# An earlier place in the queue for three transposing steps and one copy of a selective scan

## The chip, the cores and the metric

The kernel runs on one core of a Trainium2 chip. The metric is the time of one execution on the device in microseconds; the kernel before is given as the median of three runs.

## The reference

Two layers act on an input x of shape (2, 48, 48, 768) in float32, so on two images of 2304 tokens. Layer 1 adds neighbourhood attention (12 heads of 64, windows of 7 by 7) to x. Layer 2 adds a selective scan that is run over the tokens forwards and backwards:

```python
# layer 2, one direction; u, delta: (batch, 1536, 2304); A: (1536, 16); Bm, Cm: (batch, 16, 2304)
def step(h, inp):
    d_t, B_t, C_t, u_t = inp
    dA = jnp.exp(d_t[..., None] * A)
    h = dA * h + (d_t * u_t)[..., None] * B_t[:, None, :]
    y = jnp.einsum('bdn,bn->bd', h, C_t)
    return (h, y)
...
y = _selective_scan(x, delta, A, Bm, Cm) + x * Dp[None, :, None]
return y * jax.nn.silu(z)
...
out = jnp.einsum('bdl,cd->blc', out_f + out_b, out_proj_w)
```

Around it stand group norms, an input projection to x and z, a convolution of four taps, small projections that give delta, B and C, and the output projection.

## The kernel before

**Units.** The scan is cut into 288 units, numbered x = 0 to 287 in the order of execution: for each image, the forward direction and then the backward one; in each, 6 chunks of 384 tokens; in each chunk, 12 tiles of 128 channels (the change's title calls such units tiles). Units 0 to 71 are image 0 forwards, 72 to 143 image 0 backwards, 144 to 215 and 216 to 287 the same of image 1. `scan` writes the steps of one unit, and its inner `group` those of each of the 4 groups of 4 states:

1. *fill* (L1224): hb = u times B, 4 states side by side in one buffer `hb`, on VectorE or on GpSimd, whichever is free first for groups 1 to 3 (group 0 has no choice);
2. *exponentials* (L1246, ScalarE) into one of two PSUM buffers `da`;
3. *scans* (L1257, VectorE), two instructions a group, in place in `hb`;
4. *product* (L1272, GpSimd): hb times C, in place;
5. *add_up* (L1289, TensorE): 12 transposes that add the 4 states into one PSUM bank `py`. Only when they have run is `hb` free for another fill. There are seven `hb` buffers.

Each unit begins in `py` with *direct* (L1305, three transposes of x times D) and ends with a copy to `yt` (L1315, ScalarE). There is one `py`, so the next unit's *direct* waits for that copy. In the backward direction *sums* (L1342) transposes the forward result `yl` and `yt` back into one PSUM bank `yb` of the kind `mm`, of which there are two; VectorE multiplies it by the gate (L1352).

**Jobs.** All other work (attention, projections, norms, x_proj) is cut into jobs that are placed beside the scan. The attention of image 0 alone runs ahead of it. A projection is issued in parts of three products (L382), into the same two `mm` banks.

**The planner.** Nothing is ordered by hand. Every step is given to `Order.add` with an engine, an estimated duration and a *key*, its due place counted in units: a step of unit x has a key between about x - 1.4 and x + 1.4, and a job has a key that says beside which unit it should run. `Order.run` then plays the program through on its own clocks and, for each engine, takes the next step from those that are ready and whose buffers are free:

```python
                    rank = (max(t + over, free[e] + 150.0), x.first)
                    if pick is None or rank < pick[0]:
                        pick = rank, t, x
```

Here `t` is when the step could start, `free[e]` when the engine is free. All that could start within 150 ns of the engine's being free tie, and the lowest `x.first` goes ahead. It is set in `Order.add`:

```python
        x.then, x.ready, x.tail, x.first = [], 0.0, self.TAIL[eng], key - early
```

With `early` at 0 a job that is late (its key is lower than that of the unit now being scanned) goes ahead of a step of the scan. `EARLY = 20` is already given to the steps that make delta. The order that comes out is the order of issue on each engine, fixed when the program is built. A step with `alt` (the fill) may go to either engine, so a different order elsewhere can change the split. Where TensorE would stand idle for over 800 ns within a unit, transposes of a constant (L1489) are put in.

Keys that matter below, for image 0: the input projection of chunk i has keys from 9(i-1)-4 to 9(i-1)+8, its gate part for chunk 0 (`mm_z`) from 41 to 47, and the backward x_proj (`mm_xd`) from 44 to 55. For image 1: the attention has keys 50 to 118, the input projection of its first chunk 118 to 128, and its scan begins at unit 144. The output projection of image 0 has keys 188 to 212.

Of the kernel before, what the change touches and what calls it, by code (L numbers as in the profile page):

```python
# [43 lines left out]
SG = 4  # L44
# [49 lines left out]
class Order:  # L94
# [15 lines left out]
    @staticmethod  # L110
    def cells(uses):
        for x in uses:
            buf, parts = x if isinstance(x, tuple) else (x, range(x.parts))
            for p in (parts,) if isinstance(parts, int) else parts:
                yield buf, p
# [130 lines left out]
def tile_kernel(  # L246
# [3 lines left out]
    nc = tc.nc  # L250
# [57 lines left out]
    def cols(l0, cl, k0=0, nk=1):  # L308

        c0, c1 = l0 // CW, (l0 + cl) // CW  # L310
        return [k * NCW + c for k in range(k0, k0 + nk) for c in range(c0, c1)]
# [7 lines left out]
    def sb(tag, shape, n, parts=1):  # L319
        return Buf(f"{tag}_{n}", wk, shape, tag, BUFS.get(tag, 1), parts)  # L320

    def ps(tag, n):
        return Buf(f"{tag}_{n}", psum, [P, 512], tag, BUFS.get(tag, 1))
# [5 lines left out]
    def add(eng, ns, fn, key, r=(), w=(), job=False, size=0, after=None, early=0, alt=None, due=False, opens=None):  # L329

        news = [x[0] if isinstance(x, tuple) else x for x in w]

        def issue():
            for v in news:
                if v.ap is None:
                    v.ap = v.pool.tile(v.shape, F32, tag=v.tag, name=v.name, bufs=v.bufs)
            fn()

        if eng == "PE":

            ns *= 1.04 if key < 0 else 1.05
        return order.add(eng, ns, issue, key, r, w, job, size, after, early, alt, due, opens)
# [4 lines left out]
    def act(n, pointers=0):  # L347
        return 60 + 90 * pointers + n * 0.833

    def dve(n):  # L350
        return 55 + n * 1.042
# [695 lines left out]
    def x_proj(b, back, l0, cl, key):  # L1047

        n = f"{b}_{back}_{l0}"
        w = sb("xpw", [P, ND, XD], n)  # L1050
        u = staged(us[back][b], l0, cl, f"u{n}", key, w, par[back]["xpT"])
        acc = ps("mm", f"xd_{n}")
        product(acc, cl, [(w, k, 0) for k in range(ND)], [(u, k, 0) for k in range(ND)], key, XD)
        xd_out(b, back, l0, cl, n, acc, key)
# [124 lines left out]
    def scan(ch, k, x, dlj, duj, vt):  # L1179

        q, b, back, l0, cl, bc = (ch[v] for v in ("q", "b", "back", "l0", "cl", "bc"))
        at = x
# [8 lines left out]
        if k == 0 and ch["first"]:  # L1191
# [10 lines left out]
            early=EARLY,  # L1202
        )

        nt = -(-cl // P)
        tb = [slice(t * cl // nt, (t + 1) * cl // nt) for t in range(nt)]
        tp = cl // nt
        py = ps("py", n)

        def group(g):  # L1210
            m = f"{n}_{g}"
            now = at + 0.25 * g
            hb = sb("hb", [P, SG * W], m, SG + 1)
            body = (hb, range(SG))
            kept = lambda o: state[:, k, 2 * SG * g + o : 2 * SG * (g + 1) + o].rearrange(
                "p (j e) -> p j e", e=2
            )
            was = zero if ch["first"] else kept(0) if back else kept(1)

            def first():
                by, on = (dus[:, ju, :], nc.gpsimd) if filled.eng == "POOL" else (du[:, :W], nc.vector)
                on.tensor_mul(  # L1224
                    cells(hb, SG), by.unsqueeze(1).to_broadcast([P, SG, W]), bc[g].ap
                )

            if k == 0 or not ch["first"]:
                add(
                    "ACT", 98, lambda: nc.scalar.copy(bc[g][:, :, ends], was), now - 0.4,  # L1230
                    [(state, k * NSG + g)], [(bc[g], 1)], early=EARLY,
                )
            on = {"DVE": dve(SG * W), "POOL": SG * W * 2.2 + 20}
            main, other = ("DVE", "POOL") if g in (0, 1) else ("POOL", "DVE")
            filled = add(
                main, on[main], first, now - (0.35 if main == "POOL" else 0.1),
                [du, duj, bc[g]], [hb], after=marks.get(marks["n"] - 6),
                alt=(other, on[other]) if g in (1, 2, 3) else None,
            )

            def step(j):
                i = g * SG + j
                da = das[j // 2 % 2]
                add(
                    "ACT", act(cl, 1) + 45,
                    lambda: nc.scalar.activation(  # L1246
                        cells(da, 2)[:, j % 2, h], dl[:, jd, c], AF.Exp, scale=q["A"][:, k, i : i + 1]
                    ),
                    now + 0.06 * j - 0.06, [dlj], [(da, j % 2)], due=True,
                )  # L1250

            def two_steps(j):
                da = das[j // 2 % 2]
                at2 = (slice(None), slice(j * W, (j + 2) * W))
                mark = add(
                    "DVE", (4 * W + 42) / 0.96,
                    lambda: nc.vector.tensor_tensor_scan(  # L1257
                        flip(hb[at2]), flip(da[:, : 2 * W]), flip(hb[at2]), 0.0, ALU.mult, ALU.add
                    ),
                    now + 0.06 * j, [da], [(hb, (j, j + 1, SG))],  # L1260
                )
                marks[marks["n"]] = mark
                marks["n"] += 1

            for j in range(0, SG, 2):
                step(j)
                step(j + 1)
                two_steps(j)

            add(  # L1270
                "POOL", SG * cl * 2.03 + 10,
                lambda: nc.gpsimd.tensor_mul(  # L1272
                    cells(hb, SG)[:, :, h], cells(hb, SG)[:, :, h], bc[NSG + g][:, :, c]
                ),
                now + 0.25, [body, bc[NSG + g]], [body],
            )
            if not ch["final"]:
                add(
                    "ACT", 90,
                    lambda: nc.scalar.copy(  # L1280
                        kept(0)[:, :, 1:2], cells(hb, SG)[:, :, leaves : leaves + 1]
                    ),
                    now + 0.3, [body, (hb, SG)], [(state, k * NSG + g)],
                )

            def add_up():
                for j in range(SG):
                    for t in range(nt):
                        nc.tensor.matmul(  # L1289
                            py[:tp, t * P : (t + 1) * P], cells(hb, SG)[:, j, h][:, tb[t]], ident,  # L1290
                            start=False,
                            stop=g == NSG - 1 and j == SG - 1 and t == nt - 1,
                            is_transpose=True, skip_group_check=True,
                        )

            add(
                "PE", SG * nt * 109 + 60, add_up, now + 0.45, [body, py], [py],
                opens=False if g == NSG - 1 else None,
            )

# [6 lines left out]
                    is_transpose=True, skip_group_check=True,  # L1307
                )

        add("PE", nt * 109 + 60, direct, at + 0.3, [vt], [py], opens=True)  # L1310
        for g in range(NSG):
            group(g)
        yt = sb("yt", [P, CL], n)
        w, y0 = nt * P, l0
        add("ACT", act(w), lambda: nc.scalar.copy(yt[:tp, :w], py[:tp, :w]), at + 1.22, [py], [yt])  # L1315
        here = cols(l0, cl, k)
        if not back:
            add(
# [8 lines left out]
        yl, zs = (sb(v, [P, CL], n) for v in ("yl", "zs"))  # L1327
# [9 lines left out]
        yb = ps("mm", f"yb_{n}")  # L1337
# [7 lines left out]
                        skip_group_check=True,  # L1345
                    )

        add("PE", 6 * 109, sums, at + 1.28, [yl, yt, zs], [yb])
        (y, yk) = ch["ys"][k] if ch["ys"] else (zs, None)
        into = lambda: y[:, c] if yk is None else y[:, yk, c]  # L1350
        add(
# [62 lines left out]
        "po": ("mm",), "vw": ("w",) * 3, "ev": ("ev",),  # L1414
    }
    LATE = 4
    HEAD = ("bc4", "bc5", "bc6", "bc7", "bc0", "bc1")
    A0, A1, P1 = (-56, -16), (50, 118), 118
    norms, norms0, stats = [], [], []
# [6 lines left out]
    for b in range(nb):  # L1426
# [3 lines left out]
        for i in range(NCH):  # L1430
# [3 lines left out]

            if b and i < LATE:
                in_proj(b, i, start, end, gate=False)
            elif i:
                in_proj(b, i, start, end)
            else:
                take, last = x_proj_of(b, 0, i, das[0], start - 1)  # L1440
                in_proj(
                    b, i, start, end, gate=False, nk=2, tags=HEAD, banks=("mm", "mm", "py", "du"),
                    proj=take,
# [7 lines left out]
        for j, ch in enumerate(reversed(range(NCH))):  # L1451
            for h, (l0, cl) in enumerate(reversed(PIECES[ch])):
                x_proj(b, 1, l0, cl, f + (46 if b else 44) + 2 * j + h)
            if b and ch < LATE:
                in_proj(b, ch, f + 62 + 12 * j, f + 71 + 12 * j, conv=False)
# [18 lines left out]
    for x, (p, b, back, i, k) in enumerate(units):  # L1474
        if x % KB == 0 and x + KB < len(units):
            ahead(x + KB)
        scan(chunks[p], k, x, *deltas.pop(x))
        if x == len(units) - 1:
            ch = chunks[p]
            last_out_proj(b, ch["l0"], ch["cl"], ch["ys"], x - 1, x + 3)  # L1480
        elif back and k == ND - 1:
            for h, (l0, cl) in enumerate(PIECES[i]):
                at = x + 2.5 + 5 * h if b else 188 + 2 * (2 * (NCH - 1 - i) + h)
                out_proj(b, l0, cl, at, at + (4.5 if b else 1.8))
# [55 lines left out]
```

## Time and profile before

| what | value |
|---|---|
| median of three runs | 7138.75 us (7138.43 to 7145.83) |
| the profiled execution, its own time | 7136.52 us |
| its span in the profile | 7134.7 us |
| first fill of the scan | about 1051 us after the span's start |
| busy over the span: TensorE, VectorE, GpSimd, ScalarE | 6368.7, 6076.3, 5435.1, 5032.7 us |
| mean granted TensorE clock | 0.969 |

The profiled execution lies within 2.3 us of the median and 1.8 us over its own span, so sums made against the span carry over to the median. The engine names in the profile are PE (TensorE's matmuls), PEld (its weight loads), DVE (VectorE), ACT (ScalarE), POOL (GpSimd) and SPq (the queue that issues DMAs). Groups of instructions are told by line, tile and shape; a wait is told as "engine, tile, line <- what released it: us in total, times, longest". A float32 product of the program appears as two matmul instructions.

### The profile page before, as it was taken

To read this page: it belongs to the slowest core of one execution; us is meant where nothing else is said; L and a number is where in the kernel's file an instruction comes from. 1 tells how busy PE (TensorE), PEld (TensorE's weight loads), DVE (VectorE), ACT (ScalarE), POOL (GpSimd) and SP (SyncE) were. 2 spreads that over 40 slices of the span, in tenths; PEclk is the share of its full clock that TensorE was granted. 3 is DMA by queue.
4 is the path that set the end of the run, shared out by engine and by line. 5 is a ranking of instruction groups with operands and counts; after the bars stand their busy time and mean duration, and the time that the engine had idled before them with its cause. 6 is when DMAs were issued, how large, how long until landed. Compare 5 with 4: busy or idle time off the path is not lost. (4 is left out here: it accounts for less than half of the span.)

```text
span 7134.7 us, 106084 instructions
## 1 busy us (share of the span) xinstructions
PE 6368.7 (89%) x38270; PEld 4910.8 (69%) x38270; DVE 6076.3 (85%) x6222; ACT 5032.7 (71%) x11020; POOL 5435.1 (76%) x1946
## 2 busy tenths in 40 slices
PE   7999988888899999999889888888888898899888
PEld 5666656666667767777666666666678887777777
DVE  1353548998888998989899999999999999999998
ACT  1332348888887787878888677778877667778775
POOL 0000018889888989988878799899899999999997
PEclk9999989999999999999999999999999999999999
DMA  6565453444456454554443453343466676655553
GB/s 190 172 201 178 130 165 118 140 150 130 153 159 204 137 156 140 166 176 121 127 144 108 134 178 101 106 129 113 133 179 195 173 217 196 182 165 169 158 172 109
DMA packets 1338085, 1101.35 MB, mean 154 GB/s; under 512 B 136712, under 2 KB 1327800, under 8 KB 1337528
## 3 DMA queue, kind: packets, MB, share of 16 engines
q1 hardware_dynamic: 1337560, 1094.57, 51.4%
q8 instruction: 303, 4.96, 0.3%
q14 instruction: 222, 1.82, 0.1%
HBM read 881.41 MB, written 213.57 MB: 153 GB/s over the span
## 5 line engine op out<-in xcount | busy, mean ns | idle before, releaser
L1257 DVE TENSOR_TENSOR_SCAN hb<-da,hb 128x772 f32<-128x772 f32 x2304 | 3925.3, 1746 | 226.7 <-ACT da L1246 197.5
L1272 POOL TENSOR_TENSOR hb<-hb,bc 128x1536 f32<-128x1536 f32 x1152 | 3654.8, 3187 | 472.1 <-DVE hb L1257 393.3
L1246 ACT ACTIVATE da<-dlt,A 128x384 f32<-128x384 f32 x4608 | 2675.6, 584 | 948.9 <-DVE hb L1257 880.4
L1289 PE MATMUL py<-ident,hb 128*128 128x128 f32 x13824 | 1756.0, 281 | 165.5 <-POOL hb L1272 163.7
L1289 PEld LDWEIGHTS py<-ident,hb 128*128 128x128 f32 x13824 | 1601.2, 145 | 346.8 <-POOL hb L1272 245.9
L1224 POOL TENSOR_TENSOR hb<-u,bc 128x1544 f32<-128x1544 f32 x490 | 1568.3, 3202 | 25.6 <-PE py L1289 19.2
L1224 DVE TENSOR_TENSOR hb<-du,bc 128x1544 f32<-128x1544 f32 x662 | 1150.1, 1744 | 75.6 <-ACT du L1201 37.8
L1174 POOL TENSOR_TENSOR u<-dlt,u 128x384 f32<-128x384 f32 x288 | 263.7, 918 | 537.0 <-DMA dtw<-dtT 412.8
L382 PE MATMUL mm_z<-xc,w_z 128*128 128x384 f32 x1728 | 606.7, 492 | 16.1 <-ACT uz_z L955 8.4
L382 PE MATMUL mm_xin<-xc,w_x 128*128 128x390 f32 x1656 | 595.8, 503 | 25.5 <-DVE uz_u L935 15.4
L1489 PE MATMUL py<-ident 128*128 128x128 f32 x4550 | 577.8, 281 | 0.0
L382 PE MATMUL mm_out<-stage_y,w_o 128*128 128x192 f32 x3168 | 542.4, 329 | 17.7 <-DVE xr L1078 11.1
L1489 PEld LDWEIGHTS py<-ident 128*128 128x128 f32 x4550 | 529.5, 145 | 32.9 <-issue 31.4
L382 PEld LDWEIGHTS mm_out<-stage_y,w_o 128*128 128x128 f32 x3168 | 517.6, 191 | 33.3 <-DVE xr L1078 14.7
L382 PEld LDWEIGHTS mm_xin<-xc,w_x 128*128 128x128 f32 x1656 | 313.3, 195 | 250.2 <-issue 37.0
L901 POOL MEMSET xc<- 128x18 f32 x4 | 0.5, 120 | 633.6 <-DVE sm L779 633.6
L382 PEld LDWEIGHTS mm_z<-xc,w_z 128*128 128x128 f32 x1728 | 319.1, 191 | 226.9 <-ACT uz_z L955 16.4
L935 DVE SCALAR_TENSOR_TENSOR uz_u<-mm_xin,conv_w,uz_u 128x384 f32<-128x384 f32 x792 | 427.4, 606 | 42.6 <-ACT uz_u L928 38.3
L382 PE MATMUL mm_qk<-xc_xn,w_qk 128*128 128x384 f32 x1296 | 453.6, 497 | 9.7 <-DVE sm L779 2.8
L1305 PE MATMUL py<-ident,vt 128*128 128x128 f32 x864 | 163.0, 301 | 280.2 <-ACT yt L1315 279.9
L382 PEld LDWEIGHTS mm_qk<-xc_xn,w_qk 128*128 128x128 f32 x1296 | 239.1, 193 | 169.7 <-issue 16.6
L1305 PEld LDWEIGHTS py<-ident,vt 128*128 128x128 f32 x864 | 101.9, 148 | 348.0 <-ACT yt L1315 331.1
(163 smaller groups left out, 6992.0 us busy)
## 6 DMA issues: line engine op xcount, KB each, us to landing
w_o<-in_w_opT SPq DMA_DIRECT2D x264, 384.0 KB
bc<-xdf SPq DMA_DIRECT2D x96, 768.0 KB
bc<-xdb SPq DMA_DIRECT2D x96, 768.0 KB
w_qk<-in_w_qkv SPq DMA_DIRECT2D x144, 384.0 KB
w_x<-in_w_inT SPq DMA_DIRECT2D x144, 384.0 KB
w_z<-in_w_inT SPq DMA_DIRECT2D x144, 384.0 KB
w_ao<-in_w_out SPq DMA_DIRECT2D x72, 384.0 KB
u<-uf SPq DMA_DIRECT2D x48, 576.0 KB
```

Source lines behind the costliest of these rows:

```text
L382: nc.tensor.matmul(acc[:m, o0 : o0 + cl], wb[:, wi, wo : wo + m], xb[:, xi, xo : xo + cl], start=c == 0, stop=c == n - 1,)
L901: nc.gpsimd.memset(xc[:, :, : a - lo], 0.0)
L935: nc.vector.scalar_tensor_tensor(u, px[:, at[j] : at[j] + cl], q["conv_w"][:, k, j : j + 1], u, ALU.mult, ALU.add,)
L1174: lambda j=j: nc.gpsimd.tensor_mul(u[:, j, h], dl[:, j, c], u[:, j, h]), at + 0.06 + 0.25 * j,
L1224: on.tensor_mul(cells(hb, SG), by.unsqueeze(1).to_broadcast([P, SG, W]), bc[g].ap)
L1246: lambda: nc.scalar.activation(cells(da, 2)[:, j % 2, h], dl[:, jd, c], AF.Exp, scale=q["A"][:, k, i : i + 1]),
L1257: lambda: nc.vector.tensor_tensor_scan(flip(hb[at2]), flip(da[:, : 2 * W]), flip(hb[at2]), 0.0, ALU.mult, ALU.add),
L1272: lambda: nc.gpsimd.tensor_mul(cells(hb, SG)[:, :, h], cells(hb, SG)[:, :, h], bc[NSG + g][:, :, c]),
L1289: nc.tensor.matmul(py[:tp, t * P : (t + 1) * P], cells(hb, SG)[:, j, h][:, tb[t]], ident, start=False, stop=g == NSG - 1 and j == SG - 1 a ...
L1305: nc.tensor.matmul(py[:tp, t * P : (t + 1) * P], vt[:, tb[t]], ident, start=t == 0, stop=False, is_transpose=True, skip_group_check=True,)
L1489: nc.tensor.matmul(marks["py"][:, CL : CL + P], ident, ident, start=False, stop=False, is_transpose=True, skip_group_check=True,)
```

## The change

Four steps are given `early=FIRM`, with `FIRM = 4.0`: *direct*, *add_up*, the copy to `yt`, and *sums*. In the planner each is then ranked as if it were due 4 units sooner: it goes ahead of a job unless the job is late by more than about 4 units. No instruction is added, removed or altered; durations, buffers and dependencies stay. The product with the gate (L1352), the stores and all jobs keep their rank.

```diff
-                "PE", SG * nt * 109 + 60, add_up, now + 0.45, [body, py], [py],
+                "PE", SG * nt * 109 + 60, add_up, now + 0.45, [body, py], [py], early=FIRM,
                 opens=False if g == NSG - 1 else None,
...
-        add("PE", nt * 109 + 60, direct, at + 0.3, [vt], [py], opens=True)
+        add("PE", nt * 109 + 60, direct, at + 0.3, [vt], [py], early=FIRM, opens=True)
...
-        add("ACT", act(w), lambda: nc.scalar.copy(yt[:tp, :w], py[:tp, :w]), at + 1.22, [py], [yt])
+        add("ACT", act(w), lambda: nc.scalar.copy(yt[:tp, :w], py[:tp, :w]), at + 1.22, [py], [yt], early=FIRM)
...
-        add("PE", 6 * 109, sums, at + 1.28, [yl, yt, zs], [yb])
+        add("PE", 6 * 109, sums, at + 1.28, [yl, yt, zs], [yb], early=FIRM)
...
     LATE = 4
+    FIRM = 4.0
```

## The prediction, made before the changed kernel was run

> **What bounds the kernel now.** I read first the page's busy times and slices.
>
> ```profile
> PE 6368.7 (89%) x38270; PEld 4910.8 (69%) x38270; DVE 6076.3 (85%) x6222; ACT 5032.7 (71%) x11020; POOL 5435.1 (76%) x1946
> ...
> DVE  1353548998888998989899999999999999999998
> ```
>
> PE has the highest share, yet 577.8 us of it are the constant transposes of L1489, which only fill gaps. From the seventh slice on, where the scan begins, it is DVE that is full. In stretches of twelve units it is idle 22% of the time in units 36 to 47, 5 to 12% in the other stretches up to unit 143 but for 48 to 71 (2 to 3%), and 2 to 8% after. What the change can win is therefore DVE idle time of the scan, some 410 us (6065 us from the first scan to the end, less 5651 busy), and no more than the part that *add_up*, *direct* or the copy cause. The costliest groups give the prices.
>
> ```profile
> L1257 DVE TENSOR_TENSOR_SCAN hb<-da,hb 128x772 f32<-128x772 f32 x2304 | 3925.3, 1746 | 226.7 <-ACT da L1246 197.5
> L1272 POOL TENSOR_TENSOR hb<-hb,bc 128x1536 f32<-128x1536 f32 x1152 | 3654.8, 3187 | 472.1 <-DVE hb L1257 393.3
> ...
> L1224 POOL TENSOR_TENSOR hb<-u,bc 128x1544 f32<-128x1544 f32 x490 | 1568.3, 3202 | 25.6 <-PE py L1289 19.2
> L1224 DVE TENSOR_TENSOR hb<-du,bc 128x1544 f32<-128x1544 f32 x662 | 1150.1, 1744 | 75.6 <-ACT du L1201 37.8
> ```
>
> A fill costs DVE 1.74 us or POOL 3.20 us. Most DVE idle before a scan is put down to ACT's exponentials (197.5 us), which the change doesn't rank. Then the waits, longest first in total:
>
> ```profile
> PE py L1305 <- ACT yt L1315: 279.9, 144, 9.2
> ...
> DVE hb L1257 <- ACT da L1246: 197.5, 134, 5.8
> ...
> DVE hb L1224 <- PE py L1289: 34.6, 6, 28.6
> ...
> POOL hb L1224 <- PE py L1289: 19.2, 11, 4.3
> ```
>
> The third row is the one to open: six waits of DVE for *add_up*, one of them 28.6 us long. The timeline around it:
>
> ```profile
> 2133.51 5.97 PE L382 MATMUL mm_z<-xc,w_z 128*128 128x384 f32 x18
> ...
> 2145.16 11.78 PE L382 MATMUL mm_z<-xc,w_z 128*128 128x384 f32 x36
> ...
> 2158.22 4.10 PE L382 MATMUL mm_xd<-stage_u,xpw 128*80 128x192 f32 x24 [1.28 <-DMA xpw<-in_x_proj_w_b]
> ...
> 2166.03 1.47 PE L1289 MATMUL py<-ident,hb 128*128 128x128 f32 x12
> ...
> 2167.61 1.76 DVE L1224 TENSOR_TENSOR hb<-du,bc 128x1544 f32<-128x1544 f32 x1 [28.61 <-PE py L1289]
> ```
>
> From 2133 to 2166 us PE ran jobs alone, the products waited for *add_up*, all seven `hb` were held, and DVE stood still. This is at units 47 and 48, and the jobs have keys 43.5 to 46.5 (`mm_z`) and 44 to 45 (`mm_xd`): late, but by under 4 units.
>
> To see how common that is I paired the k-th product with the k-th twelve transposes of L1289 in the trace. From a product's end to the first transpose took 5.9 us on average (6781 us over 1152); in units 0 to 11 10.2, 36 to 47 15.1, 72 to 83 12.6, 84 to 95 15.9, but 1.0 to 3.4 in units 144 to 191 and 240 to 287. Counting `hb` from fill to last transpose, all seven are held for only 7, 13, 12, 1, 8 and 2% of the windows 1071-2000, 2000-3000, 3000-3927, 3927-5000, 5000-6000 and 6000-7071 us. DVE is idle while seven are held for 79 us in all, POOL for 101 us; of DVE's 79, 39.5 fall into units 36 to 47, 26.5 into 72 to 95, 4 into 0 to 11. **That, and not the 6781 us of delay, is what an earlier add_up can give back**: a filled buffer waits 4 to 8 us for its scan anyway, so a buffer that comes free a few us earlier mostly lengthens that wait.
>
> **What the Trainium skill says.** "TensorE: Matmul & The Clock Gate", Part 2 (step by step), says that matmuls keep program order and only weight loads are pulled ahead; so a transpose behind a job waits for it, as the trace agrees (32 us of jobs ahead of the transposes at 2166.03). "Perfetto Trace Analysis", Optimization Strategy, says that consistent bubbles can mean too little buffer space; here seven held buffers explain 79 of about 410 us of DVE's idle time. "SBUF — State Buffer", Who interferes with whom, says that a DVE instruction with at most one SBUF input outside its two-port modes doesn't contend with GpSimd; scan and DVE fill read one operand from PSUM, and both span only 1732 to 1768 ns in the trace, so more fills on POOL should not slow DVE.
>
> **The change part by part.** Nothing is added or removed, so busy times stay but for the split of fills.
>
> *add_up* (1152 times 1.47 us on PE). It passes jobs late by under about 4 units. Of the lateness before, read from keys against the order of issue: jobs are 2 to 5 units late in units 0 to 23, 4 to 6 in 24 to 45, under 4 for most of 46 to 71, around 1 for the attention's projections in 72 to 107 beside 6 to 18 for its cores, 15 and more in 108 to 135, within 3 or ahead in 144 to 191, 3 to 17 in 192 to 229, and within 4 after. So the rule bites in about half of the scan, and where it bites most it meets the 28.6 us stall. First term: that stall goes, **-28.6 us**. The jobs in it are still PE's to do: about 32 us of them shift to units 48 to 71, where PE is idle or on filler for (223 - 202 + 6) + (237 - 217 + 11) = 58 us; so they are covered, and late next is the start of image 1's attention, by up to one unit. Second term: the other 50 us of DVE idle with seven held. Nearly half belongs to jobs more than 4 units late, which still go first: I take **-18 us** (bounds 0 and -50). Third: POOL's idle with seven held, 101 less the 28 of the stall, half of it: 36 us are 11 more fills on POOL, 11 x 1.74 = 19 us off DVE, of which I count half, **-10 us** (bounds 0 and -40).
>
> *direct* and the copy to `yt`: the copy (0.47 us) passes jobs on ACT, chiefly a silu with its two table loads (1.28 + 2.13 + 1.28 us), never one already begun. It can shorten the 279.9 us for which PE waits at *direct*. PE is not the bound there, so I count nothing; cover is PE's own idle time. The copy ahead of an exponential can cost a scan 0.47 us; a pair of exponentials (1.17 us) has 0.57 us of room beside a scan (1.74), which covers it. Bounds: -10 and, at a tenth of the 288 copies uncovered, +14.
>
> *sums* (six transposes, about 0.9 us): takes an `mm` bank earlier and holds it until the gate product, whose rank isn't raised. Behind it wait the jobs' products for that bank. 0, bounds -5 and +15. On SP nothing is re-ranked; the stores of `yf` follow the copy and come earlier.
>
> *Jobs.* PE is never left idle by the rule, so a job loses at most the transposes pending, seven buffers or 7 x 1.47 = 10 us, at a time. That matters for one chain: image 1's attention ends late now (its norm is made at 3999.9 us, in unit 136, against a key of 118), then come the input projection, x_proj (its last store is issued at 4148.9) and the load of `dt` for unit 144 at 4176.1. Allowing some 2 us for the store to land, an estimate from the DMAs in the trace, about 25 us are free there. I charge **+10 us** for a later start of the attention against a scan that arrives earlier.
>
> Sum: -28.6 - 18 - 10 + 10 = -47 us. Against the profiled execution (7136.5) that is 7090, against the median 7092; I round the smaller terms down and say **7095 us**.
>
> **The rivals.** *No change (7139, between 7125 and 7153; chance 0.14).* The stall moves rather than goes: the 32 us of jobs meet the next units, buffers are seldom full elsewhere, and half of the late jobs are past 4 units. For it: seven held in only 1 to 13% of the time, and 197.5 us of waits for ACT that stay. Against it: PE's idle time in units 48 to 71.
>
> *Slower (about 7173; chance 0.33).* Image 1's first scan waits. The attention's core has a long chain of short PE steps through the two `mm` banks; each now yields to transposes while under 4 units late, and so do the projections that it reads, while *sums* takes one of its banks. PE is busy 242 of 258 and 257 of 271 us in units 72 to 95, with 2 us of filler, so nothing catches up there. Lateness that grows by the whole 4 units is 4 x 22 = 88 us at the rate of those units; less 25 us free and the 28.6 us of the stall it costs +34 us. It decides against the change from a delay of about 25 + 29 = 54 us at unit 144. Against it: cores 1 to 5 are already over 4 units late and keep their place. A fresh order with other single stalls of that size would look alike.
>
> *Large gain (about 7040; chance 0.08).* Units 0 to 47 and 72 to 95 drop towards their calmer neighbours: units 36 to 47 take 25.0 us each, 24 to 35 take 22.8 (26 us over twelve); 84 to 95 take 22.6, 96 to 107 20.6 (24 us); with the bounds of POOL's fills that comes to about -100.
>
> **How the numbers follow.** About 0.2% (14 us) is what a measurement of this kernel can tell from no change. Faster by more 0.53 (0.45 for the forecast, 0.08 for the large gain), within it 0.14, slower by more 0.33. The forecast's own range is 7040 to 7120. The whole reaches from the large gain, 7035, to the slower case with a second stall of some 15 us, 7188; that leaves out 2 in 10.
>
> **What would show it.** Right: no DVE wait over 10 us at units 47 and 48; the delay from product to transposes down by half or more in units 36 to 71 and still long in 108 to 135 and 192 to 229; POOL fills up from 490; PE's wait at *direct* below 279.9 us. Wrong: the load of `dt` for unit 144 following right upon the last x_proj store, with DVE idle ahead of it; or DVE's idle time unchanged, with its waits for `da` grown by what the buffers gave back.

## The result, and the profile after

The changed kernel takes 7153.22 us, the median of 20 runs (7142.81 to 7171.76), beside 7142.20 (7129.96 to 7150.35) of the kernel before on the same chip: a ratio of **1.0019, 95% interval 1.0013 to 1.0025**. I had forecast a clear gain of 44 us; it moved 11 us the other way, about the 0.2% that I had put as no change. Its profiled execution has a span of 7150.4 us against 7134.7. I begin with the page: span, busy times, and DVE's slices.

```profile
span 7150.4 us, 105844 instructions
...
PE 6377.8 (89%) x38189; PEld 4898.4 (69%) x38189; DVE 6089.5 (85%) x6229; ACT 5032.0 (70%) x11020; POOL 5414.0 (76%) x1939
...
DVE  1353449998889989998899999999999999999998
```

DVE is busy 13.2 us more than before, and its idle time from the first scan on went from 424 to 427 us. (The prediction's some 410 took 6065 us from the first scan to the end; it is 6081 us, of which 426 are idle. Counted gap by gap up to DVE's last instruction it is 424, and that count serves for both kernels.) So nothing was won on the engine that bounds the scan. The groups say what DVE has more of:

```profile
L1257 DVE TENSOR_TENSOR_SCAN hb<-da,hb 128x772 f32<-128x772 f32 x2304 | 3926.0, 1747 | 230.2 <-ACT da L1246 204.1
L1272 POOL TENSOR_TENSOR hb<-hb,bc 128x1536 f32<-128x1536 f32 x1152 | 3653.6, 3184 | 525.7 <-DVE hb L1257 458.1
...
L1224 POOL TENSOR_TENSOR hb<-u,bc 128x1544 f32<-128x1544 f32 x483 | 1545.5, 3201 | 22.2 <-PE py L1289 18.9
L1224 DVE TENSOR_TENSOR hb<-du,bc 128x1544 f32<-128x1544 f32 x669 | 1162.1, 1743 | 58.1 <-ACT du L1201 46.5
```

Each operation takes what it took. POOL has 483 fills, not 490; the seven went to DVE, 7 x 1.743 = 12 us. And the waits:

```profile
PE py L1305 <- ACT yt L1315: 225.8, 122, 8.5
...
DVE hb L1257 <- ACT da L1246: 204.1, 142, 10.2
...
POOL hb L1224 <- PE py L1289: 18.9, 13, 2.9
...
DVE hb L1224 <- PE py L1289: 7.1, 7, 2.6
```

The changed ranks do what they say. DVE's wait for *add_up* fell from 34.6 to 7.1 us, its longest from 28.6 to 2.6; PE's wait at *direct* fell from 279.9 to 225.8; the delay from a product to its transposes fell from 6781 to 5609 us over the 1152 groups, 5.9 to 4.9 us each. Yet all seven `hb` are held for 437 us in all, as before (441). At units 47 and 48, where 33 us of jobs had run alone, the timeline now reads (start, duration, engine):

```profile
2136.47 4.13 PE L382 MATMUL mm_xd<-stage_u,xpw 128*80 128x192 f32 x24
...
2141.13 1.47 PE L1289 MATMUL py<-ident,hb 128*128 128x128 f32 x12
...
2142.44 2.10 PE L382 MATMUL mm_z<-xc,w_z 128*128 128x384 f32 x6
...
2144.38 2.78 PE L1289 MATMUL py<-ident,hb 128*128 128x128 f32 x24
...
2147.00 4.04 PE L382 MATMUL mm_z<-xc,w_z 128*128 128x384 f32 x12
...
2147.26 1.74 DVE L1224 TENSOR_TENSOR hb<-du,bc 128x1544 f32<-128x1544 f32 x1
```

The same jobs, with transposes between them and a fill that waits for nothing. **So the stall went and the total didn't move down.** Where it went is seen when DVE's time is cut at the first scan of units 36, 48, ... and each stretch split by what DVE did (us, worked out from the two traces; what the lead holds beside idle time and job work is fills, +11.7 us in the end):

| units | DVE idle, before | DVE idle, after | DVE work other than scans and fills, change | lead of the changed kernel at the end of the stretch |
|---|---|---|---|---|
| 0 to 35 | 77 | 81 | +1.4 | -5 |
| 36 to 47 | 65 | 34 | -0.1 | 23 |
| 48 to 71 | 13 | 32 | -3.5 | 11 |
| 72 to 95 | 58 | 26 | -6.9 | 48 |
| 96 to 119 | 40 | 59 | +6.3 | 27 |
| 120 to 143 | 39 | 53 | -3.7 | 5 |
| 144 to 191 | 46 | 50 | +7.6 | -11 |
| 192 to end | 88 | 96 | +0.1 | -16 |

The lead reaches 48 us at unit 96 and is gone by unit 192. Idle time that leaves units 36 to 47 is back for more than half in 48 to 71 (+19), where DVE waits longer for ACT's exponentials and for its copy of delta times u (8.1 + 1.5 us before, 18.5 + 7.7 after). What leaves 72 to 95 (-32) is back in 96 to 143 (+32).

What was passed shows in image 1's attention. Its norm, before and after:

```profile
3999.86 3.18 POOL L1272 TENSOR_TENSOR hb<-hb,bc 128x1536 f32<-128x1536 f32 x1 [2.12 <-DVE gnrb L484]
3999.89 3.17 DVE L485 SCALAR_TENSOR_TENSOR gnsb<-gn_mb,gnrb 128x6 f32<-128x6 f32 x1
```

```profile
4025.45 0.17 DVE L485 SCALAR_TENSOR_TENSOR gnsb<-gn_mb,gnrb 128x6 f32<-128x6 f32 x1
```

And on SP, the last x_proj store for unit 144 and the load of `dt` that needs it, before and after:

```profile
4148.93 0.42 SPq L1040 DMA_DIRECT2D xdf<-ev  x1
...
4176.06 0.43 SPq L1369 DMA_DIRECT2D dt<-xdf  x1
```

```profile
4187.52 0.41 SPq L1040 DMA_DIRECT2D xdf<-ev  x1
4188.68 0.27 SPq L1369 DMA_DIRECT2D dt<-xdf  x1
```

The norm starts 25.5 us later (before, it lasted 3.17 us in place of 0.17, and ended within 0.02 us of the GpSimd product that had begun just ahead of it; by its end it is 22.6 us later). The store is 38.6 us later, and the load follows 1.2 us after the store where it had 27: the free time that I counted is used up. That is the sign that the prediction named as proof against it, short of its last part: unit 144 itself still begins a little earlier (4261.0, then 4255.2 us), so no scan waits at the door. PE had little room to make the attention good on the way, as the windows over units 72 to 83, 84 to 95 and 96 to 107 show (bounds, length, then busy time of PE, PEld, DVE, ACT and POOL, clock, DMA share and GB/s):

```profile
2629.00:2875.00 246.00, 230.23 (x1474) 171.56 (x1474) 234.71 (x225) 200.05 (x483) 222.53 (x80) 0.98 0.50 150
2875.00:3121.00 246.00, 230.19 (x1456) 169.25 (x1453) 231.46 (x217) 204.77 (x525) 218.97 (x79) 0.97 0.49 147
3121.00:3395.00 274.00, 259.19 (x1707) 195.64 (x1706) 238.65 (x241) 215.20 (x561) 231.25 (x83) 0.98 0.53 164
```

PE is busy 94 or 95% of each, with filler in only 4.6 us of the first and none in the others. In the second window all seven buffers are held for 22.7 us (81.9 before), in the third for 113.9 (11.8 before): the jobs put off in the second were by then about 4 units behind, so that some of them went first again, and *add_up* waited there.

### The profile page after: what moved, and what is told of

It reads as the page before. It is cut to its first block, busy times and chain, and to the rows that moved or that the text cites. A ratio compares the mean times of both kernels' runs of the same rounds, so it can differ in the third digit from the quotient of the medians.

```text
span 7150.4 us, 105844 instructions
## 1 busy us (share of the span) xinstructions
PE 6377.8 (89%) x38189; PEld 4898.4 (69%) x38189; DVE 6089.5 (85%) x6229; ACT 5032.0 (70%) x11020; POOL 5414.0 (76%) x1939
## 4 chain that ended last, share of the span: by engine, by line
DVE 39%; PE 21%; ACT 20%; issue 9%; DMA 6%; POOL 4%; SPq 1%; DVEq 0%; POOLq 0%; ACTq 0%
DVE hb L1257 27%; DVE hb L1224 6%; ACT da L1246 6%; PE mm_qk L382 4%; DVE uz_u L935 4%; PE py L1289 3%; POOL hb L1272 3%; PE mm_v L382 2%; PE mm_ao L382 2%; PE mm_xin L382 2%; ACT L1162 1%; ACT L1161 1%; ACT L962 1%; POOL hb L1224 1%; ACT uz_u L928 1%
## 5 line engine op out<-in xcount | busy, mean ns | idle before, releaser
L1257 DVE TENSOR_TENSOR_SCAN hb<-da,hb 128x772 f32<-128x772 f32 x2304 | 3926.0, 1747 | 230.2 <-ACT da L1246 204.1
L1289 PE MATMUL py<-ident,hb 128*128 128x128 f32 x13824 | 1774.1, 282 | 196.9 <-POOL hb L1272 193.5
L1224 POOL TENSOR_TENSOR hb<-u,bc 128x1544 f32<-128x1544 f32 x483 | 1545.5, 3201 | 22.2 <-PE py L1289 18.9
L1224 DVE TENSOR_TENSOR hb<-du,bc 128x1544 f32<-128x1544 f32 x669 | 1162.1, 1743 | 58.1 <-ACT du L1201 46.5
L382 PE MATMUL mm_z<-xc,w_z 128*128 128x384 f32 x1728 | 604.8, 490 | 12.7 <-ACT uz_z L955 4.6
L382 PE MATMUL mm_out<-stage_y,w_o 128*128 128x192 f32 x3168 | 556.8, 330 | 14.0 <-ACT dlt L1156 5.1
L1490 PE MATMUL py<-ident 128*128 128x128 f32 x4469 | 561.4, 279 | 0.0
L935 DVE SCALAR_TENSOR_TENSOR uz_u<-mm_xin,conv_w,uz_u 128x384 f32<-128x384 f32 x792 | 427.9, 607 | 55.2 <-ACT uz_u L928 48.7
L382 PEld LDWEIGHTS mm_xin<-xc,w_x 128*128 128x128 f32 x1656 | 308.8, 193 | 232.7 <-issue 21.9
L1305 PE MATMUL py<-ident,vt 128*128 128x128 f32 x864 | 162.5, 300 | 226.4 <-ACT yt L1315 225.8
L785 ACT ACTIVATE pr<-pr,sm 128x308 f32<-128x308 f32 x432 | 234.5, 544 | 125.7 <-DVE sm L779 125.4
```

The lines of the kernel that those rows point to most:

```text
L382: nc.tensor.matmul(acc[:m, o0 : o0 + cl], wb[:, wi, wo : wo + m], xb[:, xi, xo : xo + cl], start=c == 0, stop=c == n - 1,)
L785: nc.scalar.activation(pr[j].ap, pr[j].ap, AF.Exp, bias=sm[:, j : j + 1], scale=-1.0, accum_out=sm[:, 2 + j : 3 + j],)
L935: nc.vector.scalar_tensor_tensor(u, px[:, at[j] : at[j] + cl], q["conv_w"][:, k, j : j + 1], u, ALU.mult, ALU.add,)
L1224: on.tensor_mul(cells(hb, SG), by.unsqueeze(1).to_broadcast([P, SG, W]), bc[g].ap)
L1257: lambda: nc.vector.tensor_tensor_scan(flip(hb[at2]), flip(da[:, : 2 * W]), flip(hb[at2]), 0.0, ALU.mult, ALU.add),
L1289: nc.tensor.matmul(py[:tp, t * P : (t + 1) * P], cells(hb, SG)[:, j, h][:, tb[t]], ident, start=False, stop=g == NSG - 1 and j == SG - 1 a ...
```

## The experiments

Each ratio is to the kernel before on the same chip, with its 95% interval. In the expectations, "A" is the theory that the lead is borrowed from image 1's attention and paid back, "B" its rival, that ranks in the later units cost time by themselves (for `only_add`, `only_sums` and `no_sums` it is put anew), and "C" that one order differs from another by chance. Each run is a single order, and the last group of runs finds 0.2 to 0.6% between orders that differ by a hair, so smaller differences between totals are not read as effects.

**Where the ranks apply.** One edit in `scan`, with `early=firm` on all four steps:

```diff
+        firm = FIRM if x < 144 else 0      # lt144; in lt60: x < 60
```

> FIRM only in units 0 to 143 (image 0); units 144 to 287 ranked as before. Against the kernel before (about 7142 us). Theory A, debt: jobs that are passed are only deferred, the lead won at unit 47 is paid back before image 1's scan at unit 144 and a remainder after it, so the time is that of the change, +5 to +15 us, with the same loss after unit 144. Theory B, a rank that costs in itself: the 21 us that the changed kernel loses from unit 144 to the end (2874 to 2895 us) come from the ranks there and are gone, so -10 to -5 us. Theory C, scatter: the order before was a lucky one and any other order lands somewhere within 20 us of it, mostly above.

> FIRM only in units 0 to 59. A: a lead of about 25 us at unit 60 (the 28.6 us stall gone), gone again at unit 144 since image 1's attention starts later, end within 10 us of the kernel before. The step of the prediction that counted the stall as saved for good: -20 to -28 us at the end. C: a lead of 25 us at unit 60 and no rule after it, +-20.

Measured: `lt144` 7151.06 us, 1.0022 (1.0012 to 1.0032), as the whole change; `lt60` 7139.63 us, 1.0003 (0.9995 to 1.0011). So ranks in image 1's half cost nothing that shows; in the trace of `lt144`, units 144 to 191 take 1030 us without ranks there, as with them (1028; 1011 before). B falls. The second run keeps the cure of the stall (units 36 to 47 take 270 us, 300 before), delays no norm of image 1 (it comes 7 us earlier after the first scan than before), and still ends level with the kernel before. Its lead is 23 us at unit 48, 7 at 72, 5 at 120, -14 at 144 and 3 at 192. Its total alone refutes nothing: it is 12 us below the mean of the four orders with the old ranks (1.0020, below), which is within their scatter. The stages say more: **16 of the 23 us are lost within 24 units** (units 48 to 71 take 477 us, 458 to 461 in those four orders), with DVE idle 33 us there against 11 to 14.

**One step at a time.** `only_add` ranks *add_up* alone, `only_sums` *sums* alone, `no_sums` all but *sums*:

```diff
-        add("PE", 6 * 109, sums, at + 1.28, [yl, yt, zs], [yb], early=FIRM)
+        add("PE", 6 * 109, sums, at + 1.28, [yl, yt, zs], [yb])
```

> Only add_up keeps FIRM; direct, the copy to yt and sums are ranked as before. A: like the whole change, 0 to +15 us, since add_up is what passes jobs. B: add_up ahead of jobs makes the jobs later, and the unranked sums (backward units alone) then waits behind them and holds yt and py; no loss in units 0 to 71, then over 30 us lost in units 72 to 143. C: +-20.

> Only sums keeps FIRM. Units 0 to 71 have no sums, so the stall at units 47 and 48 and everything up to unit 71 stay as before. A: nothing is deferred by much (six transposes a unit), within 5 us. B: if sums takes mm banks that jobs need, +10 to +20 us, lost in units 72 to 143 and 216 to 287; if it was sums that was late, -5 to -15 us. C: +-20.

> FIRM on add_up, direct and the copy to yt, not on sums. Against the kernel before (about 7140 us). If add_up ahead of jobs starves the unranked sums (theory B, after the run with add_up alone, which lost 106 us, nearly all of it in units 72 to 119): +60 to +100 us, lost in units 72 to 119 again, nothing in units 0 to 71. If it was the unranked direct that cost add_up alone so much: +10 to +20, as the whole change.

Measured: `only_add` 7243.85 us, 1.0155 (1.0141 to 1.0169); `only_sums` 7142.02, 1.0008 (1.0000 to 1.0016); `no_sums`, which was run after `only_add` was known, 7242.19, 1.0143 (1.0129 to 1.0157). The size was the surprise: B had put "over 30 us" for `only_add`. *add_up*'s rank, alone or with *direct* and the copy, **costs some 105 us**, and the rank of *sums*, worth nothing that shows by itself, gives nearly all of it back. The waits of `no_sums`:

```profile
PE py L1305 <- ACT yt L1315: 294.3, 168, 12.4
...
POOL hb L1224 <- PE py L1289: 41.8, 18, 8.2
...
DVE hb L1224 <- PE py L1289: 23.2, 15, 4.0
...
ACT yt L1315 <- PE mm_yb L1342: 22.3, 15, 13.7
```

The last row stands at 0.5 us, once, for the kernel before, and is not among the waits of the changed one: the copy to `yt` waits for *sums*. I followed it to the timeline of PE at unit 76:

```profile
2739.78 2.84 PE L1289 MATMUL py<-ident,hb 128*128 128x128 f32 x24
...
2757.23 4.80 PE L382 MATMUL mm_v<-w_v,xc_xn 128*128 128x128 f32 x30
...
2769.74 0.55 PE L1342 MATMUL mm_yb<-ident,yl 128*128 128x128 f32 x3 [0.77 <-ACT ev_v L629]
2770.13 0.49 PE L1342 MATMUL mm_yb<-ident,yt 128*128 128x128 f32 x3
2770.77 0.88 PE L856 MATMUL mm_po<-pT,uz_kv 110*64 110x128 f32 x12 [0.15 <-ACT pT L832]
2771.58 0.55 PE L1305 MATMUL py<-ident,vt 128*128 128x128 f32 x3
...
2772.78 2.40 PE L1289 MATMUL py<-ident,hb 128*128 128x128 f32 x20
```

Unit 76's last transposes end at 2742.6 us. Its copy can't run, because the one `yt` still holds unit 75 until *sums* has read it; *sums*, unranked, stands behind the projections and attention steps that *add_up* has made late. It ends at 2770.6, the copy starts at 2770.65, and only then come *direct* and *add_up* of unit 77. For 28 us the ranked transposes waited behind an unranked step, through `yt` and `py`, of which there is one each. (PE keeps to its order of issue, as the Trainium skill's "TensorE: Matmul & The Clock Gate", Part 2, says of matmuls: *sums* is issued after the jobs at 2757 to 2769 us, and waits its last 0.77 us for an `mm` bank that one of them held.) Counted over the backward units, a copy counts as held if it starts within 0.6 us of the end of *sums* though its own *add_up* had ended before, and is held from that end on. ACT does other work meanwhile, so that the row of its waits shows only 22.3 us of it.

| kernel | copies held by *sums* | held for, us | mean from the copy's end to the transposes of `yt` in *sums*, units 72 to 95, us |
|---|---|---|---|
| before | 8 | 51 | 14.2 |
| `only_sums` | 2 | 4 | 8.2 |
| changed | 6 | 43 | 9.1 |
| `only_add` | 27 | 300 | 21.9 |
| `no_sums` | 34 | 334 | 21.8 |

In `no_sums` all seven buffers are held for 430 of the 1115 us of units 72 to 119. The prediction had *sums* at nothing, with bounds of -5 and +15.

**The dose.** `FIRM = 6.0` and `FIRM = 2.0`:

> FIRM = 6 in place of 4 on all four. Theory A, debt: jobs settle about 6 units late in place of 4 and image 1's attention with them; its norm (3999.9 us before, 4025.4 in the changed kernel) comes at 4050 to 4080 us, image 1's scan starts later, +30 to +60 us on the kernel before. Theory C, scatter among orders: about the changed kernel's time, +15 with 20 either way, whatever the norm's time.

> FIRM = 2 in place of 4 on all four. Theory A: the stall goes as with 4; image 1's attention falls back by less, its norm between 4000 and 4025 us; total 0 to +12 us on the kernel before. C: +-20.

Measured: `firm6` 7174.55 us, 1.0049 (1.0035 to 1.0063); `firm2` 7138.49, 0.9995 (0.9988 to 1.0001). The attention's norm moves with the dose: 3999.9 us with none, 4007.6 with 2, 4025.4 with 4, and with 6

```profile
4055.29 1.54 DVE L485 SCALAR_TENSOR_TENSOR gnsb<-gn_mb,gnrb 128x6 f32<-128x6 f32 x1
```

That fits A, though orders with the old ranks alone spread from 3970 to 4026 us (below). That the time follows the dose would fit too, but `f2_91` below takes it back for a dose of 2.

**The attention let through.** `att_too` is the changed kernel with the same rank for the TensorE steps of image 1's attention:

```diff
-                    [(*oT[k], 0) for k in range(NP)], key, job=job,
+                    [(*oT[k], 0) for k in range(NP)], key, job=job, early=FIRM * job,
...
-            add("PE", mm(1, NKEY) * 1.2, scores, key, r=[(ks, 0), qs], w=[*sc, *pr], **S)
+            add("PE", mm(1, NKEY) * 1.2, scores, key, r=[(ks, 0), qs], w=[*sc, *pr], early=FIRM * job, **S)
```

(and likewise for its other products, the turned probabilities and the weighted sum.)

> The changed kernel, with the same 4 units given also to the TensorE steps of image 1's attention (its products, scores, transposes and weighted sums), so that the transposes of the scan no longer pass these, but still pass the input projections and x_proj. Theory A: the stall at units 47 and 48 stays gone (lead 20 to 25 us at unit 48), the attention is back in time (norm of image 1 at 4000 or before, against 4025.4 in the changed kernel and 3999.9 before), but TensorE has no spare time in units 48 to 107, so now the scan loses the lead there: starts of unit 96 and 144 within 20 us of the kernel before, total within +-20 of it. If it was only the order that was bad and TensorE had room: lead kept, -15 to -30 us.

Measured: 7162.87 us, 1.0037 (1.0024 to 1.0049). The norm is back, earlier than before:

```profile
3980.12 1.28 DVE L485 SCALAR_TENSOR_TENSOR gnsb<-gn_mb,gnrb 128x6 f32<-128x6 f32 x1
```

and the lead has gone with it: 23 us at unit 48, 5 at 72, 11 at 96, none at 120, with DVE idle 50 us in units 72 to 95 (26 in the changed kernel, 58 before). So what the changed kernel won in units 72 to 95 was PE time of the attention. The orders with the old ranks, described below, show the same exchange: units 72 to 95 take 543 us with the norm at 3970 us, 527 to 529 with it at 3996 to 4000, and 496 and 504 with it at 4026 and 4022. Why it is slower than the changed kernel's 1.0019 I can't say; after the next group of runs it need not have a cause of its own.

**Less work to put off.** `before_light` and `after_light` leave out half of the products of image 1's q, k and v, in the kernel before and in the changed one:

```diff
-[(xn, c, m * P) for c in range(NC)],
+[(xn, c, m * P) for c in range(3 if job else NC)],
```

> The kernel before with half of the products of image 1's q, k and v left out (three of six input tiles), as the base for the same cut in the changed kernel: TensorE gets some 220 us less work in units 48 to 107. All theories: 20 to 40 us faster than the kernel before, since image 1's attention comes earlier.

> The changed kernel with the same half of the products of image 1's q, k and v left out. A: with room on TensorE the passed jobs are caught up with, so the lead won at unit 47 (about 25 us) is kept past unit 144: 15 to 30 us faster than the kernel before with this cut. B and C: no such gain, 5 to 20 us slower than the kernel before with this cut, as in the full kernels.

Measured: 7119.49 us, 0.9972 (0.9961 to 0.9984), and 7115.96, 0.9962 (0.9949 to 0.9975). The sign is A's, 3.5 us between the medians, but A had put 15 to 30. The intervals overlap, and 3.5 us is less than lies between two orders, so it decides nothing.

**How much does any new order move?** The change rebuilds the order of every engine, so the question is what a rebuilt order costs with the same ranks. `null_sem`, `b89` and `b92` are the kernel before with the planner's allowance for a semaphore changed (`SEM = 90.0` to 91, 89 and 92 ns); `null_rank` is the changed kernel with `FIRM = 0.1`. None alters a rank by more than a tenth of a unit. `a89`, `a91` and `a92` are the changed kernel with the same allowances, and `f2_91` is `firm2` with 91.

```diff
-    SEM = 90.0
+    SEM = 91.0
```

> The kernel before with the planner's semaphore latency at 91 in place of 90 ns: no rank is changed, only the clocks on which the order is planned. It shows how far an order that differs for no reason lies from the kernel before. Theory C: 10 to 30 us off, mostly slower. A and B say nothing, but would want it within 10 us, so that 11 us of the change can be told from scatter.

> FIRM = 0.1 on all four: a tenth of a unit, so only near ties are turned. Another measure of scatter. C: 10 to 30 us off, mostly slower. A: within 10 us, with image 1's norm at 4000 us within 10.

> The kernel before, planned with a semaphore latency of 89 ns in place of 90; ranks as before. If the order of the kernel before is one of many alike (theory C): 7125 to 7170 us, most likely above it, as with 91 ns (+0.21%). If the 91 ns order was an exception: within 5 us of the kernel before.

> The changed kernel planned with 89 ns. Compared with the kernel before planned with 89 ns: if the rank costs 11 us in itself, +5 to +20 us on that; if it is worth nothing (debt and scatter), within 10 us of it; if the rank gains but the kernel before was a lucky order, -10 to -30 us.

> The changed kernel planned with 91 ns. As the run with 89 ns, to be set beside the kernel before planned with 91 ns (7157 us): cost in itself 7162 to 7177, nothing 7147 to 7167, gain 7127 to 7147.

> The changed kernel planned with 92 ns, to be set beside the kernel before planned with 92 ns, which runs next: cost in itself +5 to +20 us on it, nothing within 10 us, gain -10 to -30 us.

> The kernel before planned with a semaphore latency of 92 ns. Scatter: 7125 to 7175 us, more likely above the kernel before than below. The fourth pair with the changed kernel at 92 ns.

> FIRM = 2, planned with 91 ns. With 90 ns it was level with the kernel before (ratio 0.9995). If that was a property of 2 units: 7130 to 7150 us again. If scatter: 7145 to 7175 us.

| allowance | ranks of before | ranks of the change | difference |
|---|---|---|---|
| 89 | 1.0027 (1.0017 to 1.0038) | 1.0036 (1.0022 to 1.0051) | +0.0009 |
| 90 | 1 | 1.0019 (1.0013 to 1.0025) | +0.0019 |
| 91 | 1.0021 (1.0012 to 1.0029) | 1.0020 (1.0014 to 1.0027) | -0.0001 |
| 92 | 1.0031 (1.0020 to 1.0042) | 1.0017 (1.0010 to 1.0023) | -0.0014 |

`null_rank` stands at 1.0028 (1.0018 to 1.0037) and `f2_91` at 1.0053 (1.0041 to 1.0065). An order that differs from the kernel before by one nanosecond in one constant of the planner is 15 us slower. **All four other orders with its ranks, `null_rank` counted in, are 0.21 to 0.31% above it**, so its own order is a lucky one among its like, and the changed kernel's +0.19% is no more than another order costs without the change. With ranks of 2 units the spread is wider still: `firm2` and `f2_91`, again one nanosecond apart, differ by 0.58%, 41 us. In the traces `f2_91` takes 1533 us for units 48 to 119, `firm2` 1486. The four differences have a mean of +0.0003 and a standard error of 0.0007 (four values, so a 95% interval of about -0.0019 to +0.0026): the ranks by themselves are worth nothing that shows.

The four pairs also show where the time goes without the luck of one order. The means of the four traces, in us:

| | ranks of before | ranks of the change |
|---|---|---|
| units 0 to 35 | 828.8 | 832.5 |
| units 36 to 47 | 299.3 | 270.5 |
| units 48 to 71 | 460.2 | 471.8 |
| units 72 to 119 | 1053.1 | 1041.7 |
| units 120 to 143 | 586.9 | 591.6 |
| units 144 to 191 | 1003.6 | 1024.8 |
| units 192 to the end | 1861.7 | 1868.4 |
| DVE idle in units 48 to 71 | 12.7 | 30.8 |
| PE idle or on filler in units 48 to 71 | 56.2 | 52.5 |
| DVE idle in units 120 to 191 | 88.7 | 103.5 |

The stall's 29 us are won in every pair. In units 48 to 71 12 us are lost (458 to 461 us in the four before, 470 to 473 in the four after, so no overlap), and in units 120 to 191 26 (again no overlap). The 7 us after them are less sure, since there the two groups do overlap. **That the lead is lost again, and in which units,** is shown in four pairs; why is shown in part only. Of the 26 us, 15 are idle time of DVE, 6 are scans and fills, and 5 are other work. Image 1's convolution (L935) keeps DVE busy 11.0 us longer in units 144 to 191 (145.6 to 155.1 us in the four before, 159.1 to 162.2 in the four after), but 10.5 us less in units 120 to 143: it has moved behind unit 144, and is hardly more work.

The attention is later as well, its norm at 3970 to 4026 us in the four before and 4025 to 4034 in the four after. The load of `dt` for unit 144 follows the last store within 1.5 us in all four after, and 20 to 78 us behind it in the four before. The convolution runs behind the input projection, which runs behind the attention; that order of steps is the code's. That the later attention is what costs the time in units 144 to 191 is not shown: `b92` has its norm at 4026 us and takes 1003 us there, and `att_too` has it at 3980 and takes 1024.

## Why the prediction was wrong, point by point

In the four pairs' traces the sum of the change is +8 us where the forecast had -47: -29 in units 36 to 47, +12 in 48 to 71, -11 in 72 to 119, +26 in 120 to 191, and +4 and +7 before and after these. (These are single executions; by the medians of all runs the four pairs differ by +2 us.)

- **"That stall goes, -28.6", saved for good.** It goes (299 to 270 us), and isn't saved. The step that failed is its cover: "PE is idle or on filler for 58 us" in units 48 to 71, so that the 32 us of jobs are covered there. The room was there and was hardly drawn on: PE idle or on filler fell by 4 us, from 56 to 52, and the stretch grew by 12. I had priced PE's time and not what DVE needs next: DVE's waits for ACT's exponentials and its copy of delta times u grew, and 19 of the 31 us of idle time came back in those very units. Why ACT's steps came late there stays open. Being ahead is not enough to explain it: `firm2` reaches unit 48 with the same lead and takes 460 us for these units. `lt60`, which ranks only units 0 to 59, loses 16 of its 23 us there too.
- **The chain of image 1, "+10".** Near the right place, and the wrong size: units 120 to 191 cost 26 us. The norm is 25.5 us later and the last store 38.6, more than the 25 us free. The step that failed is "a job loses at most the transposes pending, 10 us, at a time": the loss is renewed as long as jobs are less than about 4 units late. Read from keys against the order of issue, the middle part of a projection is 4.2 units late in units 12 to 48 (3.7 before) and 3.5 in units 84 to 95 (on time before). From about 4 units on the jobs go first again, and *add_up* waits as before. A rank of "four units" is thus a loan of up to four units, taken once. How the delay turns into the 26 us is not shown.
- ***sums* at 0.** The most mis-sized term. Without it the rest costs about 103 us (1.0143), with it 11 to 14. I looked at the bank that it takes from the jobs, and not at the buffer that it gives back: `yt` is one, and behind it stand the copy, `py`, *direct* and *add_up*.
- **"-18" for the other full buffers.** Units 72 to 95 gave 32 us of idle time, more than that; units 96 to 143 took 32 back. Over 72 to 143 DVE is idle 138 us before and after in the profiled pair (152 and 142 in the means of the four). DVE's idle time with seven buffers held, from which this term was taken, fell by 18 us in all (79 to 61), the stall included.
- **"-10" for POOL's fills.** Wrong in sign: 483, not 501 (means of the four pairs: 488 and 483). The seven lost are 12 us, which is most of the 16 us in the profiled pair.
- ***direct* and the copy at 0.** In line with the runs: PE's wait at *direct* fell by 54 us, and no gain can be traced to it. No run ranks these two alone.
- **The slower rival.** It named the delay of the attention and put the point of decision at about 54 us. The store was delayed by 38.6, and unit 144 did not wait; the time went in the stages around unit 144 and not as a wait at its door. My price of +34 was too high.
- **The bound that was missing.** I called a fresh order "with other single stalls of that size" a rider to a rival, and gave the forecast a part of its range from known terms alone. The null orders show 0.2 to 0.3% between orders with one set of ranks, up to half of my forecast, and `firm2` and `f2_91` 0.58%, nearly all of it.
- **The signs.** Of those for a gain, the long wait of DVE at units 47 and 48 went and PE's wait at *direct* fell, but the delay to the transposes in units 36 to 71 fell by 40% (7.6 to 4.6 us), not by half, and POOL's fills fell. Of those against it, the load of `dt` did follow right upon the last store, and DVE's idle time was unchanged, though its waits for `da` grew by 7 us only.
- **Small slips.** Image 1's norm was made in unit 133, by first scans, not 136. DVE is idle 13% of the last twelve units, not 2 to 8%. The parts named for the large gain (26, 24 and 40 us) add up to 90 us, not about 100. None of these moves the forecast.

Not settled, beside what is said above: why `firm6` (1.0049) and `f2_91` (1.0053) lie further up than the rest. For `firm6` the later norm is at hand; for `f2_91` with its early one (4007 us) nothing is, and either may be scatter. Nor is it known what in the kernel before makes its order a good one, beyond the place: its units 120 to 143 take 569 us, the other three orders with its ranks 587 to 599.

## What to carry to other kernels

A stall removed by letting one step pass others was here a loan: the time won was lost again in later stages. Before counting such a gain, ask which engine is full in the next stages, whose chain the passed work begins, and whether the freed engine then only waits for a third. When a step is put first, put first everything that must run before its buffers come free again; here the rank of the step that frees the single `yt` was worth some 90 us once *add_up* had been moved. And where an order is planned by machine, plan it again with a constant changed by a hair, for both versions, before a difference of some tenths of a per cent is given a cause; here a nanosecond moved the time by up to 0.58%.

## What the runs showed that I had not expected

The mean granted TensorE clock differs from kernel to kernel, and time doesn't follow it: all five runs of `firm6` have 0.972 to 0.975 and are among the slow ones, the runs of `no_sums` 0.958 to 0.962, the ten of the kernel before beside them 0.967 to 0.970. And where DVE has seven fills more and POOL seven fewer, scan and fills keep their durations to a nanosecond or two (1746 and 1747 ns; 1744 and 1743; 3202 and 3201), as the prediction took from the Trainium skill's "SBUF — State Buffer", Who interferes with whom.
